# K's bias product at full height inside the warm-up, and the shared low-rank products of gate and up in one group

## The chip, the core and the metric

One core of a Trainium2 chip runs the whole kernel. The metric is the device time of one launch in microseconds (us); every tensor is float32.

## The reference

For x of 2 x 1024 tokens and 512 features, the layer computes

```
xn  = layernorm(x)
Q,K = elu(xn wq^T + bq) + 1,  elu(xn wk^T + bk) + 1        # 16 heads of 32
V   = xn wv^T + bv
att = (Q (K^T V)) / (Q . sum(K) + 1e-8)                    # linear attention
out = x + att wo^T + bo + down(silu(gate(xn)) * up(xn))
gate, up, down = W + shared low rank (sA sB / 8) + experts' low rank (A_e B_e / 8, top 2 of 8 by a router)
```

The hidden width is 1376 = 10 x 128 + 96, the rank 8, and there are 8 experts. The shared low-rank part doesn't depend on the token, so the kernel adds sA sB to the weight itself ("folds" it) and then multiplies once.

## The kernel before, in words

Each engine's order is written out by hand for PE, DVE, ACT and POOL; a line's place in the source is its place in that engine's queue, and an engine runs its queue in order. Only the DMA queue of SP is ordered by the compiler's scheduler. The products are cut up in Strassen's manner (seven products in place of eight), so DVE and POOL build sums of weights and tokens, while PE multiplies. The stages, in order of time:

1. **Start.** PE runs `WARM` = 18 transposes of the identity (L249), while the first tile of x is loaded and normalized. The loop at L667 handles the first two tiles of 128 tokens: `moments` and `deviations` give the mean and 1/sqrt(variance) on DVE, with one square root (`sd`, L268) on ACT; `norm` (L298) writes `xn`; `transpose_x(0)` transposes `xn` on PE (L308) and copies it out of PSUM on ACT (L310). Then comes `pbk`: the row bk is spread over 128 partitions by a product of a column of ones with the row (L676), contracting over 1 row, and ACT copies it back into `bk_sb` (L677). `project_k` (L362) begins K's projection.
2. **K, and K^T times xn** (to about 134 us), for 16 tiles in pairs; the sums `pg` of L401 gather in the four PSUM banks `pg0` to `pg3`.
3. **`query_unit(0)`**: Q of the first batch. Between its products stands `Finish(1)`, which turns the second batch's `pg` into the attention's matrix. Its banks come in turn from `pg0` to `pg3`, by the counter `made`: the products are `pc`, `pr`, `pv`, two `pw` and four `pko` (L553), and ACT copies each `pko` into `gt` (L554). After it the PSUM is given out anew, eight banks in turn, and `shared_factors` transposes the shared factors (`psa`, L560) into `sat`.
4. **`query_unit(1)`**: Q of the second batch, with hooks between its products. `attend(0)` multiplies Q by the spread 1/denominator (L903); `fold_rest(0)` in hook P7 folds gate's part of the 96 last columns (`pfr` L1046 on PE, adds L1049 on DVE). Hook P4 loads the first pair of gate and up weights.
5. **The rest stage** (to about 239 us): `fold_rest(1)` for up, then `rest(b)` for each batch: three products `pr` (L1077 to L1090) of the 96 last columns, with two places for other work between them. `fold(0, 0)` and `fold(0, 1)` stand there: `fold_pe` (L958) multiplies, for four chunks of 128 features, 8 rows of `sat` with 8 rows of sB; `fold_adds` (L967) adds the results to the weights, and `fold_sums` (L971 to L974) builds the Strassen sums. `inner_weight_sums` (`wi`, L1176 to L1179) goes one level deeper.
6. **Ten units** (`unit(j, b)`), then the down projection and attention's output together, to the end.

Two kinds of PE instruction matter. Every float32 product is two passes, each with its own weight load. And where a product contracts over 8 rows only, four of them are placed on four groups of 32 rows (`rows = slice(k * 32, ...)`) and write four banks.

`hold(v)` (L145) is a small memset on DVE ahead of a load: the load then waits for DVE's place in its queue.

Of the kernel before, what the change touches and what calls it, by code (L numbers as in the profile page):

```python
# [15 lines left out]
P = 128  # L16
# [21 lines left out]
def layer_kernel(  # L38
# [23 lines left out]
    nc = tc.nc  # L62
# [10 lines left out]
    RANK = LR // (E + 1)  # L73
# [4 lines left out]
    NC = D // P  # L78
# [8 lines left out]
    REST = DFF - FULL * P  # L87
# [3 lines left out]
    UT = TB // 2  # L91
    NQ = UT // P
    NPQ = NC // 2
    WARM = 18
    NBC = 3

    TILES = [b * TPBATCH + g * TPB + t for b in range(NBATCH) for t in range(TPB) for g in range(2)]
# [1 line left out]
    def by_chunk(w):  # L99
        return w.rearrange("(c p) n -> p c n", p=P)  # L100
# [38 lines left out]
    ident = const.tile([P, P], F32, name="ident")  # L139
# [9 lines left out]
    def load_x(n):  # L149
        x_sb[n] = x_ring[:, n % 4, :]  # L150
        nc.sync.dma_start(out=x_sb[n], in_=x[ts(TILES[n], P), :])

    wk_sb = p1.tile([P, NC, D + E], F32, name="wk_sb")
    load_x(0)
    bk_sb = p1.tile([P, D], F32, name="bk_sb")
    nc.scalar.dma_start(out=bk_sb[0:1, :], in_=bk.unsqueeze(0))
    nc.scalar.dma_start(out=wk_sb[:, :, D:], in_=by_chunk(w_router))
    for c in range(NC):
# [28 lines left out]
    sat = ffn.tile([P, n_sat, P], F32, name="sat")  # L187
# [3 lines left out]
    ones = p1.tile([P, P], F32, name="ones")  # L191
# [3 lines left out]
    for b in range(NBATCH):  # L195
        t = p2.tile([P, 2, NC, 32], F32, name=f"ksd{b}")
# [43 lines left out]
    tags = None  # L240

    def bank(name, shape=None, tag=None):
        tag = tag or (next(tags) if tags else "ps")
        return ps_pool[0].tile(shape or [P, TB], F32, tag=tag, name=name)


    warm = bank("warm", [P, NC, P], "pt")
    for _ in range(WARM):
        nc.tensor.transpose(warm[:, 0, :], ident, ident)  # L249

    def moments(first, n):
        for i in range(first, first + n):
# [4 lines left out]
    def deviations(first, n):  # L257
        variances(first, n)
        reciprocals()
# [42 lines left out]
    def transpose_x(n, tag="pt"):  # L302
        i = TILES[n]
        pt = [bank(f"pt{i}", [P, NC, P], tag)] * 2
        if n == 0:
            pt[1] = bank("pt0_1", [P, NC, P], "ua")
        for c in range(NC):
            nc.tensor.transpose(pt[c // 2][:, c, :], xns[n][:, ts(c, P)], ident)  # L308
        for k in range(2):
            nc.scalar.copy(xnT[i // TPBATCH][k][:, :, ts(i % TPBATCH, P)], pt[k][:, 2 * k : 2 * k + 2, :])  # L310
# [184 lines left out]
    class Finish:  # L495


        def __init__(self, b, pg, ksum):
            self.b, self.pg, self.ksum = b, pg, ksum
            self.made = 0  # L500

        def bank(self, name, shape=None):
            if self.b == 0:
# [163 lines left out]
    for n in range(2):  # L667
        moments(n, 1)
        deviations(n, 1)
        norm(n)  # L670
        load_x(n + 4)
        if n == 0:
            transpose_x(0)

            pbk = bank("pbk", tag="x")
            nc.tensor.matmul(pbk, ones[0:1, :], bk_sb[0:1, :], start=True, stop=True)  # L676
            nc.scalar.copy(bk_sb, pbk)  # L677
    wq_sums, sums1 = query_weight_sums(), token_sums(1)
    sums0 = [take_sums(0, i) for i in range(2)]
    fin = []  # L680
# [18 lines left out]
    def load_weights(t, w):  # L699
        hold(t[:, 0, 0:1])  # L700
        nc.sync.dma_start(out=t, in_=by_chunk(w))
# [38 lines left out]
    tags = cycle(("x", "pt", "ua", "lo"))  # L740
# [146 lines left out]
    def attend(b, g=None):  # L887

        if b:
            todo = [(c, g) for c in range(NC)]  # L890
            by = []
            for c in range(NC):
                rows = slice(c * 32, (c + 1) * 32)
                by.append(bank(f"pb{b}_{g}_{c}"))
                nc.tensor.matmul(by[c], spread[rows, g, :], dens[b][rows, :], start=True, stop=True)
        else:
            k = len(attended)
            attended.extend((k, k + 1))
            todo = [(i % NC, i // NC) for i in attended[-2:]]
            by = [bcs[i] for i in attended[-2:]]  # L900
        for (c, g), t in zip(todo, by):
            v = qt[b, c, g]
            nc.vector.tensor_mul(v, v, t)  # L903
            if b == 0:
                spread_den()

            j, i = c % NPQ, c // NPQ
            nc.sync.dma_start(
                out=q_dram[b][j][:, :, 2 * i + g, :].rearrange("s p n -> p s n"),
                in_=v.rearrange("p (s n) -> p s n", n=UT),  # L910
            )
# [35 lines left out]
                )  # L947
        wsum[j] = (ws, sb)

    def fold_pe(j, i, tags=()):  # L950

        sb = wsum[j][1]
        pf = []
        for k in range(NC):
            rows = slice(k * 32, k * 32 + RANK)
            name = f"pf{i}_{j}_{k}"
            pf.append(spare_bank(tags[k], name) if tags else bank(name))
            nc.tensor.matmul(pf[k][:, 0 : 2 * P], sat[rows, i, :], sb[rows, i, :, :], start=True, stop=True)  # L958
        return pf

    def fold_adds(j, i, pf):

        t = wsum[j][0][i]
        v = t.rearrange("p s (k m) -> p s k m", m=P)
        for k in range(NC):
            at = v[:, k // 2 : k // 2 + 7 : 6, k % 2, :]
            nc.vector.tensor_add(at, at, pf[k][:, 0 : 2 * P].rearrange("p (h m) -> p h m", h=2))  # L967

    def fold_sums(j, i):
        t = wsum[j][0][i]  # L970
        nc.vector.tensor_add(t[:, S1, :], t[:, A21, :], t[:, A22, :])  # L971
        nc.vector.tensor_sub(t[:, S3, :], t[:, A11, :], t[:, A21, :])
        nc.vector.tensor_sub(t[:, S2, :], t[:, S1, :], t[:, A11, :])
        nc.vector.tensor_sub(t[:, S4, :], t[:, A12, :], t[:, S2, :])  # L974
# [19 lines left out]
    tags = None  # L994
# [8 lines left out]
    def token_diffs(b, tag):  # L1003
        xdiff.append(ffn.tile([P, TB], F32, tag=tag, name=f"xdiff{b}"))
        nc.gpsimd.tensor_sub(xdiff[b], xa[b][:, 0:TB], xa[b][:, TB:BT])

    def fold(j, i):
        def f():
            fold_adds(j, i, fold_pe(j, i))
            fold_sums(j, i)  # L1010

        return f

    RA = P // 2
    RB = REST - RA

    def rest_cols(i):

        return slice(i * RA, (i + 1) * RA), slice(P + i * RB, P + (i + 1) * RB)
# [15 lines left out]
                nc.sync.dma_start(out=sb[k * 32 : k * 32 + RANK, i, :], in_=bw[ER:LR, RC])  # L1037
        return t, sb, bd

    def fold_rest(i):  # L1040
        t, sb, _ = w_rest
        pf = []
        for k in range(NC):
            rows = slice(k * 32, k * 32 + RANK)
            pf.append(bank(f"pfr{i}_{k}"))
            nc.tensor.matmul(pf[k][:, 0:REST], sat[rows, i, :], sb[rows, i, :], start=True, stop=True)  # L1046
        for k in range(NC):
            for at, f in zip(rest_cols(i), (slice(0, RA), slice(RA, REST))):
                nc.vector.tensor_add(t[:, k, at], t[:, k, at], pf[k][:, f])  # L1049

    def rest(b, between=(None, None)):
        t, _, bd = w_rest
# [47 lines left out]
    for _ in range(2):  # L1100
# [1 line left out]
    token_diffs(0, "xd")  # L1102
    query_unit(1, {
        "P5": [lambda: attend(0)],
        "P7": [lambda: fold_rest(0), lambda: attend(0)],
        "P3": [lambda: attend(0)],
        "P4": [lambda: attend(0), lambda: load_weights(0, True)],
    })
    load_weights(1)
    def u_tile(name):  # L1110
        return up_.tile([P, TB], F32, tag="u", name=name)

# [37 lines left out]
    def token_sums_1(eng, b):  # L1150

        t = xnT[b][0][:, :, TB:BT].rearrange("p k (h n) -> p k h n", n=TH)
        b11, b21 = tsum[b][1][:, 0], tsum[b][1][:, 1]
        eng.tensor_sub(t[:, 0, 0], b11[:, TH:], b11[:, 0:TH])
        eng.tensor_sub(t[:, 0, 1], b21[:, TH:], t[:, 0, 0])
        eng.tensor_sub(t[:, 1, 0], b21[:, TH:], b11[:, TH:])
        eng.tensor_sub(t[:, 1, 1], b21[:, 0:TH], t[:, 0, 1])
        inner_tokens(b, (1,), lambda i, k: t[:, k // 2, k % 2])
# [309 lines left out]
        return sb, wdr, bd, *diffs  # L1468

    sb_d, wdr, bd_sb, wdr_diff, bd_diff = load_last()  # L1470
    fold_rest(1)
    low_rank_in(2)
    low_rank_in(3)
    denominators(1)
    list(token_sums_56(nc.vector, 0, slot(6, [2, 4, TH], "ti56_0")))
    rest(0, (fold(0, 0), lambda: attend(1, 0)))
    attend(1, 1)
    token_diffs(1, "den")
    token_sums_1(nc.vector, 0)
    rest(1, (fold(0, 1), lambda: list(inner_weight_sums(nc.vector, 0, (1, 5, 6)))))  # L1480
    flush()
    ps8.close()
    p2_stack.close()
# [35 lines left out]
    FREE = ("held0", "held1", "x0", "x1"), ("ab0", "x0", "ab1", "x1")  # L1519

    def next_pair(j):

        pf = {}


        def pe(i):
            return lambda: pf.update({i: fold_pe(j, i, FREE[i])})

        def adds(i):
            return lambda: fold_adds(j, i, pf.pop(i))  # L1530

        def sums(eng, *ps):
            return lambda: list(inner_weight_sums(eng, j, ps))

        last = {}

        def last_sums(n):
            def f():
                g = last.setdefault(0, inner_weight_sums(nc.vector, j, (1, 5, 6)))
                for _ in range(n):  # L1540
                    next(g, None)

            return f

        return (
            {"6c": [pe(0)], "1d": [adds(0)], "6d": [pe(1)], "7": [adds(1)]},
            {"6c": [lambda: fold_sums(j, 0)], "2c": [lambda: fold_sums(j, 1), sums(nc.gpsimd, 3)],
             "3b": [sums(nc.gpsimd, 2), last_sums(2)], "3d": [last_sums(3)]},
        )
# [26 lines left out]
    tags = cycle(("ab0", "ab1", "x0", "x1"))  # L1576
# [590 lines left out]
```

## Time and profile before

| | us |
|---|---|
| median of 3 runs | 726.39 |
| lowest, highest | 724.82, 728.07 |
| the profiled execution | 724.74 |
| its span (what the profile covers) | 722.9 |
| PE busy | 714.9 |
| DVE busy | 579.9 |
| ACT, POOL busy | 198.2, 143.7 |

The profiled execution lasted 1.84 us longer than the span that the profile shows. Times in the profile count from the span's start. A line of the chain of waits has the start, the length, the engine, the tile written and the source line; a line of the timeline has the start, the time from the first to the last of merged instructions, and in brackets how long the engine had been idle and what ended that.

### The profile page before, as it was taken

How to read it: one execution, taken by the hardware profiler on the slowest of the kernel's cores; microseconds unless marked ns; L12 is line 12 of the kernel's file. 1: busy time of each engine (PE TensorE's matmuls, PEld its weight loads, DVE VectorE, ACT ScalarE, POOL GpSimd, SP SyncE). 2: the span in 40 equal slices, each digit the busy share in tenths (PEclk: the TensorE clock that was granted, in tenths of full speed). 3: DMA queues.
4: the chain of work that ended last, by engine and by line, in shares of the span. 5: the costliest groups of instructions: out<-in, count | busy, mean ns of one | idle time of the engine just before them, and what ended most of it. 6: DMA issues, size and time to landing. Idle time of an engine off the chain costs nothing.

```text
span 722.9 us, 9907 instructions
## 1 busy us (share of the span) xinstructions
PE 714.9 (99%) x3428; PEld 491.3 (68%) x3428; DVE 579.9 (80%) x1330; ACT 198.2 (27%) x438; POOL 143.7 (20%) x176
## 2 busy tenths in 40 slices
PE   8999999999999999999999999999999999999998
PEld 6666675454433566567567667566688899899897
DVE  6788766777687688778878878868888889998884
ACT  4434413453442233333333333333200000000000
POOL 4033011101000771311311310544520100000000
PEclk9999999999999999999999999999999999999999
DMA  6343001115585001211201201334653344533101
GB/s 177 99 137 104 0 1 57 42 34 144 131 218 155 19 4 58 88 34 58 88 29 59 88 30 59 117 120 143 204 182 117 117 161 129 158 109 110 59 16 44
DMA packets 61734, 66.85 MB, mean 92 GB/s; under 512 B 10866, under 2 KB 49522, under 8 KB 61428
## 3 DMA queue, kind: packets, MB, share of 16 engines
q1 hardware_dynamic: 61154, 66.20, 29.9%
q8 instruction: 27, 0.44, 0.3%
q14 instruction: 23, 0.19, 0.1%
q10 hardware_dynamic: 530, 0.02, 0.0%
HBM read 44.11 MB, written 22.09 MB: 92 GB/s over the span
## 4 chain that ended last, share of the span: by engine, by line
PE 83%; DVE 13%; ACT 3%; issue 1%; DMA 0%; DVEq 0%
PE ab L1202 16%; PE b L1262 8%; PE po L1942 7%; PE pg L401 5%; PE pya L1771 4%; PE pxa L1771 3%; PE pqu L772 3%; PE pyb L1771 3%; PE ph L1639 3%; PE x L1202 3%; PE pxb L1771 2%; PE pyc L1771 2%; PE pxa L851 2%; PE b L1257 2%; PE pr L1090 2%; PE kua L430 2%
## 5 line engine op out<-in xcount | busy, mean ns | idle before, releaser
L1262 PE MATMUL b<-t,w 128*128 128x512 f32 x160 | 83.2, 601 | 0.8 <-DVE t L1284 0.8
L401 PE MATMUL pg<-kt,xn 128*128 128x512 f32 x128 | 58.7, 594 | 0.5 <-DVE kt L345 0.5
L1284 POOL TENSOR_TENSOR r<-r,r 128x512 f32<-128x512 f32 x20 | 30.1, 1525 | 84.5 <-DVE t L1284 82.9
L1202 PE MATMUL ab<-ti,wi 128*128 128x256 f32 x180 | 45.4, 379 | 0.0
L1202 PEld LDWEIGHTS ab<-ti,w 128*128 128x128 f32 x140 | 25.1, 189 | 29.4 <-DVE r L1230 8.2
L1284 DVE TENSOR_TENSOR r<-r,r 128x512 f32<-128x512 f32 x60 | 44.9, 788 | 0.0
L1202 PEld LDWEIGHTS ab<-ti,wi 128*128 128x128 f32 x180 | 34.2, 190 | 13.2 <-issue 5.0
L1202 PE MATMUL ab<-ti,w 128*128 128x256 f32 x140 | 41.2, 387 | 0.5 <-DVE r L1230 0.2
L401 PEld LDWEIGHTS pg<-kt,xn 128*128 128x128 f32 x128 | 23.2, 190 | 22.6 <-issue 20.6
L1235 ACT COPY r<-ab 128x256 f32<-128x256 f32 x50 | 18.6, 373 | 71.1 <-PE ab L1202 71.1
L1230 DVE TENSOR_TENSOR r<-r,ab 128x256 f32<-128x256 f32 x50 | 20.9, 417 | 20.1 <-ACT r L1227 19.6
L1262 PEld LDWEIGHTS b<-t,w 128*128 128x128 f32 x160 | 29.2, 190 | 11.3 <-issue 5.9
L1238 DVE TENSOR_TENSOR r<-r,ab 128x256 f32<-128x256 f32 x50 | 20.8, 417 | 16.0 <-ACT r L1235 15.7
L1212 ACT COPY r<-ab 128x256 f32<-128x256 f32 x50 | 18.7, 374 | 48.5 <-PE ab L1202 47.1
L1942 PE MATMUL po<-wd,f 128*128 128x256 f32 x140 | 30.9, 380 | 0.1
L410 POOL TENSOR_TENSOR ksum<-ksum,kt 128x512 f32<-128x512 f32 x12 | 15.8, 1318 | 71.7 <-DVE lg L447 42.3
L1223 ACT COPY r<-ab 128x256 f32<-128x256 f32 x50 | 18.6, 373 | 40.8 <-PE ab L1202 40.8
L1942 PEld LDWEIGHTS po<-wd,f 128*128 128x128 f32 x140 | 26.4, 190 | 4.4 <-issue 0.5
L1885 DVE TENSOR_TENSOR f<-f 128x256 f32<-128x256 f32 x84 | 29.3, 417 | 0.1
L1202 PE MATMUL ab<-xnT,w 128*128 128x256 f32 x100 | 29.4, 390 | 0.0
L1202 PE MATMUL ab<-xnT,wi 128*128 128x256 f32 x100 | 28.1, 379 | 0.0
L1202 PEld LDWEIGHTS ab<-xnT,w 128*128 128x128 f32 x100 | 18.1, 189 | 10.8 <-issue 4.5
(482 smaller groups left out, 1652.1 us busy)
## 6 DMA issues: line engine op xcount, KB each, us to landing
h_dram<-h SPq DMA_DIRECT2D x40, 256.0 KB
f<-h_dram SPq DMA_DIRECT2D x10, 512.0 KB
x_ring<-in_x_dram SPq DMA_DIRECT2D x16, 256.0 KB
q_dram<-qt SPq DMA_DIRECT2D x16, 256.0 KB
xr<-in_x_dram SPq DMA_DIRECT2D x16, 256.0 KB
out_dram<-xr SPq DMA_DIRECT2D x15, 256.0 KB
w<-in_w_up_dram SPq DMA_DIRECT2D x10, 256.0 KB
w<-in_w_gate_dram SPq DMA_DIRECT2D x10, 256.0 KB
```

The costliest lines, as they stand in the source:

```text
L401: nc.tensor.matmul(pg[m], xns[n][:, ts(m, P)], kt, start=(j == 0), stop=(j == TPBATCH - 1))
L772: nc.tensor.matmul(banks[c], wqs[p][:, k, ts(c, P)], tsum[b][p][:, k, :], start=(start and k == 0), stop=(k == 1), skip_group_check=True,)
L1202: nc.tensor.matmul(out, w, t, start=start, stop=True, skip_group_check=True)
L1212: nc.scalar.copy(self.r[0][:, H0], self.ua)
L1230: nc.vector.tensor_add(self.r[1][:, H1], self.r[1][:, H1], self.lo)
L1238: nc.vector.tensor_add(self.r[1][:, H0], self.r[1][:, H0], self.lo)
L1262: nc.tensor.matmul(pb[m], ws[m][:, A_OF[p], ts(k, P)], tsum[b][p][:, k, :], start=start, stop=True, skip_group_check=True)
L1284: eng.tensor_add(to[m], t[m], v[m])
L1639: nc.tensor.matmul(phs[u][g * ER : (g + 1) * ER, :], a, f[:, g, :], start=(ns[0] == 0 and n == 0), stop=(last and n == len(chunks) - 1), s ...
L1771: nc.tensor.matmul(o, lhsT, rhs, start=first, stop=True, skip_group_check=True)
L1885: op(t[:, at, :], t[:, x_, :], t[:, y, :])
L1942: nc.tensor.matmul(ps[p][:, q, :], lhsT, rhs, start=start, stop=stop, skip_group_check=True)
```

## The change

- `bk_sb` is filled with zeros by DVE before the row bk is loaded into row 0; `pbk` contracts over all 128 rows, and stands on PE after 13 warm-up transposes, with 3 more behind it, instead of behind `transpose_x(0)`. The copy of `pbk` stands on ACT ahead of the copies of `transpose_x(0)`.
- `Finish` starts its counter at 3: for the second batch `pc` takes `pg3`, `pr` `pg0`, `pv` `pg1`, the two `pw` `pg2` and `pg3`, and `pko` 0 to 3 take `pg0` to `pg3` in this order (before: `pg1`, `pg2`, `pg3`, `pg0`).
- `fold_rest` is done once for gate and up, behind `query_unit(1)`: 8 products in one group into 4 banks, and 8 adds of double width instead of 16.
- The first fold is done once for gate and up in the first place within `rest(0)`; its sums come later on DVE, behind `attend(1, 1)`; `inner_weight_sums` moves from the second place of `rest(1)` to the first.
- `load_weights(1)` gets the four `hold` memsets. In the order that the compiler then gives SP, the loads of the second pair of weights stand behind those of the first, loads of `wdr` and `bd_sb` take the places that they had, and the eight small loads of `sb` for the third pair stand ahead of the second batch's `q_dram` stores.

```diff
-    WARM = 18
+    WARM = 13, 3
...
     bk_sb = p1.tile([P, D], F32, name="bk_sb")
+    nc.vector.memset(bk_sb, 0.0)
     nc.scalar.dma_start(out=bk_sb[0:1, :], in_=bk.unsqueeze(0))
...
-    for _ in range(WARM):
-        nc.tensor.transpose(warm[:, 0, :], ident, ident)
+
+    def warm_up(n):
+        for _ in range(n):
+            nc.tensor.transpose(warm[:, 0, :], ident, ident)
+
+    warm_up(WARM[0])
+
+    pbk = bank("pbk", tag="x")
+    nc.tensor.matmul(pbk, ones, bk_sb, start=True, stop=True)
+    warm_up(WARM[1])
...
-            self.made = 0
+            self.made = NC - 1
...
         if n == 0:
+            nc.scalar.copy(bk_sb, pbk)
             transpose_x(0)
-
-            pbk = bank("pbk", tag="x")
-            nc.tensor.matmul(pbk, ones[0:1, :], bk_sb[0:1, :], start=True, stop=True)
-            nc.scalar.copy(bk_sb, pbk)
...
-    def fold_pe(j, i, tags=()):
+    def fold_pe(j, tags=(), ms=(0, 1)):
...
-            nc.tensor.matmul(pf[k][:, 0 : 2 * P], sat[rows, i, :], sb[rows, i, :, :], start=True, stop=True)
+        for i in ms:
+            for k in range(NC):
+                rows = slice(k * 32, k * 32 + RANK)
+                nc.tensor.matmul(pf[k][:, ts(i, 2 * P)], sat[rows, i, :], sb[rows, i, :, :], start=True, stop=True)
...
-    def fold_rest(i):
+    def fold_rest():
         t, sb, _ = w_rest
-        pf = []
+        pf = [bank(f"pfr{k}", [P, 2, REST]) for k in range(NC)]
+        for i in range(2):
+            for k in range(NC):
+                rows = slice(k * 32, k * 32 + RANK)
+                nc.tensor.matmul(pf[k][:, i, :], sat[rows, i, :], sb[rows, i, :], start=True, stop=True)
         for k in range(NC):
...
+            for at, f in ((slice(0, P), slice(0, RA)), (slice(P, None), slice(RA, REST))):
+                v = t[:, k, at].rearrange("p (i n) -> p i n", i=2)
+                nc.vector.tensor_add(v, v, pf[k][:, :, f])
...
-        "P7": [lambda: fold_rest(0), lambda: attend(0)],
+        "P7": [lambda: attend(0)],
...
-    load_weights(1)
+    load_weights(1, True)
...
-    fold_rest(1)
+    fold_rest()
...
-    rest(0, (fold(0, 0), lambda: attend(1, 0)))
+
+    def first_fold():
+        pf = fold_pe(0)
+        for i in range(2):
+            fold_adds(0, i, pf)
+
+    rest(0, (first_fold, lambda: attend(1, 0)))
     attend(1, 1)
     token_diffs(1, "den")
+    for i in range(2):
+        fold_sums(0, i)
     token_sums_1(nc.vector, 0)
-    rest(1, (fold(0, 1), lambda: list(inner_weight_sums(nc.vector, 0, (1, 5, 6)))))
+    rest(1, (lambda: list(inner_weight_sums(nc.vector, 0, (1, 5, 6))), None))
```

More of the change, by code (lines that the diff above doesn't have):

```diff
@@ L954, in fold_pe @@
         for k in range(NC):
-            rows = slice(k * 32, k * 32 + RANK)
-            name = f"pf{i}_{j}_{k}"
+            name = f"pf{ms[0]}_{j}_{k}"
             pf.append(spare_bank(tags[k], name) if tags else bank(name))
-            nc.tensor.matmul(pf[k][:, 0 : 2 * P], sat[rows, i, :], sb[rows, i, :, :], start=True, stop=True)
+        for i in ms:
+            for k in range(NC):
+                rows = slice(k * 32, k * 32 + RANK)
+                nc.tensor.matmul(pf[k][:, ts(i, 2 * P)], sat[rows, i, :], sb[rows, i, :, :], start=True, stop=True)
         return pf
@@ L966, in fold_adds @@
             at = v[:, k // 2 : k // 2 + 7 : 6, k % 2, :]
-            nc.vector.tensor_add(at, at, pf[k][:, 0 : 2 * P].rearrange("p (h m) -> p h m", h=2))
+            nc.vector.tensor_add(at, at, pf[k][:, ts(i, 2 * P)].rearrange("p (h m) -> p h m", h=2))
     def fold_sums(j, i):
@@ L1005, in token_diffs @@
         nc.gpsimd.tensor_sub(xdiff[b], xa[b][:, 0:TB], xa[b][:, TB:BT])
[L1007 to L1012, printed above, removed]
     RA = P // 2
@@ L1038, in rest_weights @@
         return t, sb, bd
-    def fold_rest(i):
+    def fold_rest():
         t, sb, _ = w_rest
-        pf = []
-        for k in range(NC):
[L1044 to L1049, printed above, removed]
+        pf = [bank(f"pfr{k}", [P, 2, REST]) for k in range(NC)]
[3 more added lines that the diff above has]
+                nc.tensor.matmul(pf[k][:, i, :], sat[rows, i, :], sb[rows, i, :], start=True, stop=True)
+        for k in range(NC):
+            for at, f in ((slice(0, P), slice(0, RA)), (slice(P, None), slice(RA, REST))):
+                v = t[:, k, at].rearrange("p (i n) -> p i n", i=2)
+                nc.vector.tensor_add(v, v, pf[k][:, :, f])
     def rest(b, between=(None, None)):
@@ L1526, in pe @@
         def pe(i):
-            return lambda: pf.update({i: fold_pe(j, i, FREE[i])})
+            return lambda: pf.update({i: fold_pe(j, FREE[i], (i,))})
         def adds(i):
```

## The prediction

> **What bounds the kernel now.** I read the page's busy row and the chain first. PE is busy for 99% of the span, the chain lies on PE for 83%, and DMA has none of it: only what shortens PE's queue, or a wait on that chain, counts.
>
> ```profile
> PE 714.9 (99%) x3428; PEld 491.3 (68%) x3428; DVE 579.9 (80%) x1330; ACT 198.2 (27%) x438; POOL 143.7 (20%) x176
> PE 83%; DVE 13%; ACT 3%; issue 1%; DMA 0%; DVEq 0%
> ```
>
> Then the chain of waits in the three windows that the change touches. At the start it crosses engines:
>
> ```profile
> 6.15 0.67 PE pt L308 x4
> 6.82 1.06 PE pbk L676 x2
> 7.88 0.02 issue
> 7.90 0.59 ACT bk_sb L677
> 8.49 0.11 ACT sd L268
> ```
>
> `sd` of the second tile stands behind the copy of `pbk` on ACT; the timeline has its input `ve` done at 7.96 (7.81 + 0.15), and `sd` starts at 8.38. From there DVE's statistics lead to the first `pg` at 17.18.
>
> Timeline of PE where the PSUM is given out anew, and the chain's two `pd`, and its low-rank groups:
>
> ```profile
> 163.36 1.02 PE L772 MATMUL pqv<-t,wq_sb 128*128 128x512 f32 x2
> 164.73 0.38 PE L560 MATMUL psa<-ident,sa 128*128 128x128 f32 x1 [0.36 <-ACT gt L554]
> ```
> ```profile
> 169.55 1.85 PE pd L873 x16
> ...
> 192.20 0.41 PE pfr L1046 x8
> 192.61 3.63 PE pqu L772 x8
> 196.24 3.43 PE pqv L772 x8
> 199.67 0.41 PE pfr L1046 x8
> 200.08 7.06 PE pxa L851 x16
> 207.15 2.20 PE pd L873 x16
> ...
> 218.28 0.65 PE pf L958 x8
> 218.92 1.05 PE pr L1088 x2
> 219.98 3.43 PE pr L1090 x8
> ```
>
> To see: `psa` waits for the last copy of `gt`; the same 16 passes of `pd` take 2.20 instead of 1.85; and the product behind a low-rank group is 0.20 longer than its like (3.63 to 3.43; 1.05 to two passes of 0.43). So a `pfr` group costs 0.61 in all, a `pf` group 0.84.
>
> **The change part by part.**
>
> *Start.* Removed from PE behind `pt`: 1.06. But the chain goes on through DVE, which gains only what `sd` waited for: 8.38 - 7.98 = **0.40**. PE's side: without `pbk`, K's first 12 passes (2.7 us, 7.80 to 10.53) start when the first `xnT` copy ends (6.59 + 0.37), at 7.0, and end at 9.65, before the next transposes, due at 10.53 - 0.40 = 10.13. Now the cover in the warm-up. The 18 warm transposes start 0.216 apart ((4.10 - 0.42) / 17), those at 10.53 0.11 apart ((0.60 - 0.27) / 3): PE is at half speed there, though the page's clock row reads 9 everywhere. 13 of them end at 4.17; at half speed `pbk` is two passes of 0.86, the three behind it 0.65: `pt` could start at 6.54 instead of 6.15. The Trainium skill ("TensorE: Matmul & The Clock Gate", Part 1) has full rate after about 4 us of sustained activity, give or take 0.5: 5.4 here, `pbk` ends at 5.65 and `pt` isn't late. It speaks against putting work where PE runs at half rate; but 0.39 late makes K's passes end at 10.04, still before 10.13. By the row or by the rule, 0.40.
>
> The zeros: DVE is idle until 3.27; nearest is POOL's memset of 128x640, 0.63. The row's load then issues at about 1.4 instead of 0.74; the 256 KB of x landed 2.5 us after issue, so this row lands by 3.9, before 4.17. Behind it ACT's router load and table load (1.28) end at about 3.7, before `sd` at 4.40. Cost nothing; if the row came later than 4.7 or so, `pt` would be later than the cover allows, one for one.
>
> *Counter.* `psa`'s first bank is `pg0`: last read by the fourth `gt` copy before, by the first one now (162.64 + 0.62). PE's next pass after 163.36 and its follower falls at 164.22; `psa` started at 164.73. Gain between 0.36 (the bracket) and 0.51. The fourth and fifth `psa` then wait for DVE's adds L831 of `pqv` (the second ends at 165.10), where they arrive anyway (164.22 + 0.21 + 7 x 0.11 = 165.2). I take **0.50**. `pc` now waits for the copy of `pg3`, done at 136.2, five us early; `pko`'s fourth has the same wait as before.
>
> *fold_rest.* The first group goes (0.61), the second doubles. Its second half costs columns alone, 2 x 96 at 0.43 per 512 = 0.16, or as the first half, 0.37 to 0.41. The skill ("TensorEngine Tiling (Array Packing)", Key Properties) says that a change of tiling mode drains the array, and that tiles can load weights and multiply in parallel; that would hide the loads: gain 0.45. The row says otherwise: `pf` takes 0.65 for two passes, 0.32 each, where 256 columns are 0.21, so 0.11 of load shows in each pass. Gain **0.22**, the switch alone.
>
> DVE loses eight adds at P7 (1.00 us from 193.71) and does the wide ones behind the holds (0.4 longer than the eight there, 0.93). So `attend` at P7 frees its buffer 0.9 earlier, and the load for which L903 waits 1.73 at 200.76 is issued 0.9 earlier (it follows that buffer: 195.33 on SP). `pd` waits for the last `qt` of DVE behind it (the 0.35); PE arrives 0.22 sooner, DVE 0.9: **0.35**, or 0 if the load doesn't move. The adds then end around 208.5, `pr` L1080 needs the first of them after 209.
>
> *First fold.* The group at 218.28 gets 0.65 longer, the one at 234.75 goes (0.84): **0.20** (0.41 by the rule). DVE does eight adds there (4 take 1.41) instead of four adds and four sums (2.9 us either way), so `pb` behind it waits no longer. They need the up weights: the first pair's 1 MB is issued from 209.6, ahead of the second pair, and DMA moved 270 to 304 GB/s then: landed by about 215, used at 219.5.
>
> *Sums later.* Eight sums (2.96) follow `attend(1, 1)` on DVE; behind them are `token_sums_1`, three `hr` products and `wi`, whose third step PE needs in the first unit (242.31 before, 240.6 now). DVE: 228.5 + 2.96 + 1.46 + 2.1 + 2.3 = 237.3. Free by 3.3 us.
>
> *SP and holds.* Two loads of 0.5 leave the place between `d_dram` and `bc`, two small ones of 0.6 take it: even. Eight `sb` loads (2.8) go ahead of the `q_dram` stores, which wait for DVE at 224 anyway, and end before `wi` overwrites their tile at 235. Four memsets are 0.08 on DVE; their tiles were last read at 196.
>
> Sum: 0.40 + 0.50 + 0.22 + 0.35 + 0.20 = 1.67. The ten units are untouched. The profiled execution, 724.74 (span 722.9 and 1.84 around it), becomes 723.1; it lay 1.65 under the median, so against 726.39 I expect **724.7**. With the bounds (0.36, 0 for `pd`; 0.45, 0.41 for the folds) 1.2 to 2.1.
>
> **The rivals.**
>
> *Given back:* what PE saves at `psa` and `pd` returns as a wait for `bc` or `wT`, whose loads hang on SP's queue (issuing or waiting without a gap from 164.71 to 191.28) and move only with the start. For it: L903's wait of 1.73. Against: two of the three waits are tied to DVE, not to SP. Left are 0.40 + 0.22 + 0.20: 725.6.
>
> *More:* DVE's and POOL's earlier work lifts a stall in the first unit. For it: at 253.25 two adds L1284 take 3.36 beside POOL (0.69 alone), and PE waits 0.8 for the next. POOL's chain can begin 6 us earlier. Against: its fifth step waits for stores of `hr`, so it ends only some 3 us earlier than the shift alone. With 0.8 there, 0.5 in the units behind and the folds at 0.86: 723.0, to 722.
>
> *Slower:* DVE between `attend(1, 1)` and the first unit. POOL's sums L1176 start as soon as the eight sums are done, so ten DVE steps (four token sums, three `hr`, three `wi`) may run against it at up to 1.69 instead of about 0.6 (the 3.36 / 2 above): 10 later at worst. From 3.3 on PE stands still at the first `wi` product, from 5.0 the kernel is slower than before, at the worst 6.7 - 1.7 = 5.0 slower: 731.4. Against: POOL's wait for `hr` leaves DVE alone after four steps.
>
> *Doesn't do what it says:* the two halves of a bank written one after the other by the same row group might not overlap the four groups at all: then a merged group costs 8 x 0.21 more and `pf` loses about 1 us: 725.9. The passes of one group already follow each other in the same bank, so I give it little.
>
> **How the numbers follow.** What a measurement of this kernel can tell from no change is about 0.5%, 3.6 us: below 722.8 is faster, above 730.0 slower. The sum as worked out has 0.62, given back 0.13 (with the last rival), more 0.17, slower 0.08. The runs shown spread by 1.6 to each side. Faster: most of "more" and a small part of the first, 0.20; slower: 0.05 of its case; same 0.75. The range takes the first case with its bounds and the runs' spread, and reaches into "more": 722.0 to 727.0.
>
> **What would show it.** Right: `pbk` before 6.2 and `sd` of the second tile near 8.0; `psa` straight behind `pqv`; `pd` twice about 1.85; one `pfr` group of 16 near 0.8 and one `pf` group near 1.3; PE's first `wi` product without a bracket. Wrong: `pt` later than 6.6; a bracket with `bc`, `wT` or `w` ahead of a PE product between 164 and 245; a first unit that starts less than 1.2 earlier than before.

## The result, and the profile after

The changed kernel takes **722.71 us** (median of 5 runs, 722.40 to 723.49), beside 728.07 (724.82 to 728.35) for the kernel before on the same chip: ratio 0.9941, 95% interval 0.9922 to 0.9959. The prediction was 724.7, in a range of 722.0 to 727.0. The profiled execution took 722.83 (span 721.0); before, 724.74 (722.9). The two profiles differ by 1.9 us and the two medians by 5.4. That gap is the main thing to explain.

The page's busy row and the shares of the chain, after:

```profile
PE 714.4 (99%) x3426; PEld 491.4 (68%) x3426; DVE 578.4 (80%) x1327; ACT 198.3 (28%) x438; POOL 142.6 (20%) x176
PE 85%; DVE 12%; ACT 2%; issue 1%; POOL 0%; DVEq 0%; POOLq 0%
```

PE is busy for only 0.5 us less: most of the 1.9 us is waiting that went. The chain of waits at the start:

```profile
1.37 3.04 PE warm L252 x13
4.40 1.92 PE pbk L257 x2
...
7.02 0.62 PE pt L317 x2
...
7.66 0.38 ACT xnT L319
...
8.09 2.90 PE pk L371 x12
10.98 0.44 PE pt L317 x4
...
17.47 3.70 PE pg L410 x8
```

The start did not pay in this run. Both passes of `pbk` ran at half rate, `pt` came at 7.02, and K's passes instead of DVE's statistics lead to the next transposes (10.98 in the chain, 10.82 in the timeline, where 10.13 was forecast). The first `pg` is 0.29 later than before (17.18). The first tile of x, too, landed 0.18 later than before (3.45 and 3.27), but it is not on this chain: `pt` followed PE's own warm-up.

The chain in the middle:

```profile
161.25 3.43 PE pqv L778 x8
164.69 1.27 PE psa L569 x10
...
169.39 1.85 PE pd L879 x16
...
198.91 0.63 PE pfr L1047 x16
...
206.60 1.85 PE pd L879 x16
...
217.39 1.08 PE pf L966 x16
```

`psa` follows `pqv` without a gap. The second `pd` takes 1.85 (2.20 before). One group of 16 `pfr` takes 0.63, where one of 8 took 0.41. One group of 16 `pf` takes 1.08, where one of 8 took 0.65. So the second half of a merged group costs 0.22 and 0.43. Its columns alone, two passes at 0.43 per 512 columns, are 0.16 and 0.43.

In the first unit another 0.68 went: from the `pf` group to the second `b` product behind it are 5.66 us, before 6.34. The two ends in the chain, before and then after:

```profile
251.26 0.64 PE pf L958 x8
...
257.60 1.12 PE b L1262 x2
```
```profile
249.96 0.68 PE pf L966 x8
...
255.62 1.12 PE b L1265 x2
```

In the page's list of costliest groups, of before and then of after, the wait has left the last column (idle before the engine, and what ended it):

```profile
L1262 PE MATMUL b<-t,w 128*128 128x512 f32 x160 | 83.2, 601 | 0.8 <-DVE t L1284 0.8
```
```profile
L1265 PE MATMUL b<-t,w 128*128 128x512 f32 x160 | 83.2, 601 | 0.1
```

### The profile page after: what moved, and what is told of

It reads as the page before. It is cut to its first block, busy times and chain, and to the rows that moved or that the text cites. A ratio compares the mean times of both kernels' runs of the same rounds, so it can differ in the third digit from the quotient of the medians.

```text
span 721.0 us, 9901 instructions
## 1 busy us (share of the span) xinstructions
PE 714.4 (99%) x3426; PEld 491.4 (68%) x3426; DVE 578.4 (80%) x1327; ACT 198.3 (28%) x438; POOL 142.6 (20%) x176
## 4 chain that ended last, share of the span: by engine, by line
PE 85%; DVE 12%; ACT 2%; issue 1%; POOL 0%; DVEq 0%; POOLq 0%
PE ab L1205 16%; PE b L1265 8%; PE po L1953 7%; PE pg L410 5%; PE pqu L778 4%; PE pya L1782 4%; PE pxa L1782 4%; PE pyb L1782 3%; PE ph L1650 3%; PE x L1205 3%; PE pxb L1782 2%; PE pyc L1782 2%; PE pxa L857 2%; PE b L1260 2%; PE pqv L778 2%; PE pr L1092 2%
## 5 line engine op out<-in xcount | busy, mean ns | idle before, releaser
L1287 DVE TENSOR_TENSOR r<-r,r 128x512 f32<-128x512 f32 x60 | 43.2, 762 | 0.0
```

Source lines behind the costliest of these rows:

```text
L1287: eng.tensor_add(to[m], t[m], v[m])
```

## The experiments

### The kernel before, looked at again

No edit.

> The kernel before, unchanged, with a profile of its own. Half-rate theory (in some runs TensorE stays at half speed past the warm-up and K's first products pay for it): the times spread again over about 724.8 to 728.4, and a profile of a run above 726.5 shows K's first passes (L362) about 0.43 apart instead of 0.22, a first pg later than 17.2. Even theory (the savings seen in the profile are all, the spread lies elsewhere): a slow run's profile has its first pg at 17.2 and loses its time later.

Measured: 726.41 (724.64 to 728.48, 22 runs), ratio 0.9998 (0.9988 to 1.0009). The times are not spread evenly. Of all 86 runs of this kernel in the experiments, 8 lie at 724.6 to 725.1, 39 at 726.1 to 726.7, 39 at 727.8 to 728.7, and none between. So its median depends on how many runs fall in each group (about 726.4 in four sets of runs, 728.1 in two). The profile of before that I had predicted from, at 724.74, is of the smallest group. This profile, at 726.45, is of the middle one. Its chain at the start:

```profile
6.49 0.67 PE pt L308 x4
7.16 1.05 PE pbk L676 x2
8.21 4.51 PE pk L362 x12
...
19.21 3.70 PE pg L401 x8
```

K's 12 passes take 4.51, where the sum had 2.7. The same time in windows (from:to, length, busy time and number of instructions of PE, its weight loads, DVE, ACT and POOL, then the granted clock of PE and two figures of DMA):

```profile
5.59:9.00 3.41, 2.51 (x10) 1.48 (x11) 1.98 (x8) 1.34 (x4) 1.26 (x1) 1.00 1.00 337
9.00:12.42 3.42, 3.42 (x10) 2.62 (x9) 3.16 (x10) 0.20 (x1) 3.39 (x3) 0.50 0.27 72
12.42:15.83 3.41, 3.41 (x19) 2.96 (x18) 1.84 (x8) 1.77 (x5) 0.78 (x3) 1.00 0.32 96
```

The third number from the end is the clock: full for 3.41 us, half for 3.41, full for good. With PE busy throughout, 10 passes fit into the half-rate stretch and 19 into the next. In the full-rate stretch ahead of it PE is busy for only 2.51 us, and the 1.05 of `pbk` are of a product over one row. The page's clock row reads 9 in every slice, as a slice is 18 us.

### A run of the upper group

No edit, one profiled run.

> The kernel before, for a profile of another group of runs. If it is one of the 728 group: the stretch of 3.41 us ahead of 6.2 to 7.7 us holds the idle time ahead of pt and is followed by a second at half rate, full rate comes only at 9.6 to 11.1 or at 13 to 14.5 us, and the first pg starts near 20.5 to 20.8 (17.2 in the 724.7 group, 19.2 in the 726.3 group).

Measured: 728.36, span 726.6. Its chain:

```profile
6.43 1.09 PE pt L308 x4
7.51 2.00 PE pbk L676 x2
9.51 4.89 PE pk L362 x12
...
20.89 3.70 PE pg L401 x8
```

`pt`, `pbk` and most of K's twelve passes are at half rate; the trace has full rate from 13.65. Counted back from there in stretches of 3.41, one runs from 3.41 to 6.82 and has the 0.95 us of idle time ahead of `pt`; the next, 6.82 to 10.24, has the 2.00 of `pbk` over one row. Neither was followed by full rate; the one after it, full of K's products, was. The expectation held, the first `pg` by 0.1 later than its upper end. So in the three profiled runs of this kernel (724.74, 726.45, 728.36) the first `pg` starts at 17.18, 19.21 and 20.89: 2.03 and 1.68 apart. (The runs are 1.71 and 1.91 apart, as the second `pd` takes 2.20, 1.85 and 2.06 in them.) A stretch of 3.41 at half rate can cost 1.7 us of PE's work, and these are the steps between the groups.

### Only the start

The kernel before with the start of the changed kernel (zeros, `WARM = 13, 3`, `pbk` in the warm-up, its copy ahead of `transpose_x(0)`).

> Before, with the start's part of the change alone (zeros, bias product at full height in the warm-up, copy first). Half-rate theory: the long product keeps TensorE busy until the transposes, the spread shrinks to about 1 us and the median falls by 2.5 to 4 us, to about 724 to 725.5, though the profile's first pg lies 0.3 later than in a fast run of before. Even theory: the median rises by 0.3 us and the spread stays.

Measured: 724.57 (723.9 to 725.1, 5 runs), ratio 0.9959 (0.9944 to 0.9974). The groups are gone. In its profile full rate came at 4.97, so that the second pass of `pbk` was already fast; the chain has

```profile
2.12 4.41 DMA x_ring<-in_x_dram
...
7.69 0.21 ACT sd L277
...
8.87 0.93 DVE xn L307
...
16.78 3.70 PE pg L410 x8
```

The first `pg` is 0.40 earlier than before, but the equality with the prediction's step is partly luck. `sd` follows its input (7.51 + 0.16) at once, so the wait of 0.4 is gone; besides, the second tile of x landed 0.32 earlier than in the first profile (6.54; DVE took it at 6.86 there), and `xn` behind it took 0.93 instead of 0.55.

### All but the start

The changed kernel with the start of before.

> The changed kernel, with the start as before (18 transposes, bias product of height 1 behind the first transposes). Half-rate theory: its fast runs are at 722.4 (0.3 below the changed kernel), but runs spread by over 3 us up to about 726, median 724.5 to 726. Even theory: all runs at about 722.4, as tight as those of the changed kernel.

Measured: 724.30 (722.93 to 726.05, 10 runs), ratio 0.9965 (0.9950 to 0.9980). Three groups again, at 722.9 to 723.2, 724.2 to 724.5 and 725.9 to 726.1: each about 2 us under its like of before. So the rest of the change is worth 2 us in every group, and the start is what removes the groups.

### Products in place of transposes in the warm-up

```diff
-    WARM = 18
+    WARM = 9
-        nc.tensor.transpose(warm[:, 0, :], ident, ident)
+        nc.tensor.matmul(warm[:, 0, :], ident, ident, start=True, stop=True)
```

> Before, with 9 real products of the identity in the warm-up instead of 18 transposes (the same 18 passes of 128 columns). If only products count as work for the clock: full speed comes within the warm-up in every run, its later passes are 0.11 apart, the spread shrinks, and the median is at 724 to 725. If transposes count alike, or the spread lies elsewhere: times and spread as before, 724.8 to 728.4.

Measured: 728.00 (724.78 to 728.45, 14 runs), ratio 0.9999 (0.9985 to 1.0013), the same three groups (3, 3 and 8 runs). What kind of work fills the warm-up doesn't matter here.

### Full height at the old place

```diff
+    nc.vector.memset(bk_sb, 0.0)
-            nc.tensor.matmul(pbk, ones[0:1, :], bk_sb[0:1, :], start=True, stop=True)
+            nc.tensor.matmul(pbk, ones, bk_sb, start=True, stop=True)
```

> The kernel before, with bk_sb filled with zeros and pbk contracting over all 128 rows, but at its old place behind transpose_x(0), and 18 warm transposes. Its runs and those of the kernel before fall in three groups (about 724.7, 726.3, 728.0); the profile of a 726 run has TensorE back at half rate for one stretch of 3.41 us after its first 3.41 us at full rate. Theory 'gap' (PE's idle time between the last warm transpose and pt, about 0.7 to 1.0 us, brings the half-rate stretch): height changes nothing, the groups stay, median 726 to 728, ratio 1.000 within 0.002. Theory 'height' (the product over 1 row counts for nothing in the stretch): the 726 group goes to 724.7, the 728 group, whose stretch lies ahead of pbk, stays; fastest runs in most, median 724.7 or 728, hardly a run near 726.3.

Measured: 726.26 (724.71 to 726.80, 10 runs), ratio 0.9975 (0.9965 to 0.9984): 4 runs at 724.7 to 725.5, 6 at 726.2 to 726.8, none at 728. Of before's 15 runs on the same chip 10 were there, 5 at 726.3 to 726.7 and none lower. Neither theory had this. Its profile, at 726.55, says what became of the upper group:

```profile
7.35 1.72 PE pbk L677 x2
...
19.24 3.70 PE pg L402 x8
```

Here, too, PE idled (0.79) ahead of `pt` and `pbk` ran at half rate, but full rate came at 10.36, one stretch after the idle one and not two. A reading that fits both kernels: a product over one row counts in a stretch much like idle time, one over 128 rows counts as work, and too much of the former keeps the clock at half rate or puts it back there. Then the upper group loses its second bad stretch and becomes this one at 726.3, and the old middle group loses its only one.

### No gap ahead of the transposes

```diff
-    WARM = 18
+    WARM = 22
```

> The kernel before with 22 warm transposes in place of 18, so that at half rate they end at about 6.1 us, where pt is due; the bias product stays behind pt and over 1 row. Theory 'gap': the groups at 726.3 and 728.0 go, all runs between 724.5 and 725.5 (pt may be 0.2 late in some), ratio about 0.998. Theory 'height': the 726 group stays, since its stretch holds the 1.05 us of pbk; only the 728 group goes; median 726.3 or 724.7.

Measured: 725.41 (724.76 to 726.41, 5 runs), ratio 0.9969 (0.9957 to 0.9981); 4 of 5 runs at 724.8 to 725.5, none at 728. This is nearer to "gap". The run at 726.41 may be a middle one that kept its bad stretch (the one row counting for nothing); it has no profile. Height and gap each take part.

How much a stretch may hold can be narrowed down from the profiles, by counting stretches of 3.41 us from the moment that full rate came. At half rate, with full-height work or transposes, stretches with up to 0.58 us of idle time (the run with products in the warm-up) were followed by full rate, and those with 0.78 or more (the changed kernel) were not. At full rate, 0.43 of idle time with 1.06 of the product over one row did no harm (this run; the kernel before at 724.74 is alike), while 0.90 and 0.96 with 1.05 brought half rate back, at 726.45 and in the profile of "All but the start". Idle time alone did not: a stretch of the run "The first fold in two places again", below, has as much of it, but its `pbk` is of full height and lies in the warm-up.

```profile
5.95:9.37 3.42, 2.52 (x13) 1.59 (x12) 1.87 (x7) 1.44 (x4) 0.15 (x1) 1.00 0.82 295
9.37:12.78 3.41, 3.41 (x19) 2.70 (x18) 3.20 (x10) 0.80 (x4) 3.33 (x3) 1.00 0.50 101
```

PE is busy for 2.52 here and was for 2.51 in the run at 726.45; there half rate followed, here it did not. That speaks for the height as the other part. It is one profile, and no run changed the two in small steps.

### The product earlier in the warm-up

```diff
-    WARM = 13, 3
+    WARM = 10, 3
```

> The changed kernel with 10 warm transposes ahead of pbk and 3 behind it, in place of 13 and 3. In the changed kernel's profile the clock was at half rate to 7.41 us and pt came at 7.02, 0.7 late, so that K's first passes set the next transposes at 10.98. Here pt can start at about 6.4 at half rate, and the transposes behind K's passes at 10.3 to 10.5. Theory 'late pt costs': 0.3 to 0.5 us less in the runs whose clock opens late, median 722.3, lowest as before (722.4 less 0.1). Theory 'DVE's statistics bound the start in nearly all runs': no difference, 722.7. Rival 'the row is late': bk lands after the tenth transpose, pbk waits, a gap opens on PE and half-rate stretches come back: 723.5 to 726.

Measured: 722.63 (722.28 to 723.34, 5 runs), not to be told from the changed kernel's 722.71. In the timeline of PE the product now waits for its row:

```profile
4.21 2.05 PE L257 MATMUL pbk<-bk_sb,ones 128*128 128x512 f32 x2 [0.45 <-DMA bk_sb<-in_bk_dram]
```

The row lands just before 4.2, not by 3.9 as I had worked out, so 13 transposes are barely the cover that it needs. In this run `pt` still came at 6.79 and the next transposes at 10.43 (7.02 and 10.82 in the changed kernel's timeline), but the second tile of x, which landed at 7.2, set the chain. The effect stays below the spread.

### The counter back at 0

```diff
-            self.made = NC - 1
+            self.made = 0
```

> The changed kernel with the bank counter of Finish at 0 as before. psa then waits for the last copy of gt again: a bracket of about 0.36 at psa, and 0.45 to 0.50 us more in all: 723.2, with psa 0.45 later against the end of pqv. Rival: the wait that it removes is taken up by the next one (the adds of pqv, or SP's loads for pd), then 0 to 0.1 more: 722.8.

Measured: 723.46 (722.69 to 724.04, 6 runs), 0.75 over the changed kernel's median, with spreads of 1.1 and 1.4 us. The timeline is more exact:

```profile
165.14 1.38 PE L569 MATMUL psa<-ident,sa 128*128 128x128 f32 x10 [0.37 <-ACT gt L563]
```

The bracket is back. By the chain, `pxa` behind it moves from 165.96 to 166.53, while the first `pg` moved by only 0.08 (17.47 to 17.55): 0.49 for the counter, as predicted.

### `fold_rest` in two places again

The changed kernel with the old `fold_rest(i)` put back, gate's part in hook P7.

> The changed kernel with fold_rest as before: gate's part in hook P7 of query_unit(1), up's part behind it, 8 products in each. 'Columns alone': the second pfr group costs 0.41 of its own and a switch of about 0.2 behind it, so the stretch from psa to the first pr L1079 gets 0.37 (pfr) + 0.35 (pd back at 2.20) = 0.72 longer: 723.4. 'Row' (the prediction's own): 0.22 + 0.35. Rival: pd stays at 1.85, because it was not DVE's earlier end that moved the load: 0.37 alone, 723.1. In the first unit nothing changes (the first b product still without a bracket) if that gain comes from the first fold.

Measured: 723.26 (722.43 to 724.20, 5 runs). Its chain:

```profile
192.10 0.41 PE pfr L1047 x8
192.50 3.63 PE pqu L778 x8
...
199.57 0.41 PE pfr L1047 x8
...
207.04 1.85 PE pd L879 x16
```

The group at P7 costs 0.41 and the switch behind it 0.20 again, so merging saves 0.61 less the 0.22 of the second half. But `pd` stays at 1.85, with DVE's eight adds back in P7: the rival came true. So look again at the wait of L903 for the load of `bc`, in the list of waits (instruction, releaser: total, times, longest). In the three profiles of before (the first, the run at 726.45 and the run at 728.36) it was

```profile
DVE qt L903 <- DMA bc<-d_dram: 1.7, 1, 1.7
```
```profile
DVE qt L903 <- DMA bc<-d_dram: 0.7, 1, 0.7
```
```profile
DVE qt L903 <- DMA bc<-d_dram: 1.6, 1, 1.6
```

and `pd` took 2.20, 1.85 and 2.06. The runs with this part as before fit in: a wait of 1.5 gave 1.96, of 1.0 to 1.2 gave 1.85; in the changed kernel a wait of 1.3 gave 1.85. The load lands differently from run to run of one kernel, and in these runs it reached PE only from 1.5 on.

### The first fold in two places again

The changed kernel with gate's fold and its sums in the first place of `rest(0)`, up's in the first of `rest(1)`, `inner_weight_sums` in the second.

> The changed kernel with the first fold as before: gate in the first place of rest(0), up in the first of rest(1), each with its sums at once, inner_weight_sums in the second place of rest(1). 'Columns alone': the two groups cost 0.41 more on PE; and the first unit: if the 0.68 there comes from POOL's and DVE's earlier sums of the first fold, it goes as well, with a bracket of 0.6 to 0.8 at the second b product: 1.1 in all, 723.8. Rival: the first unit's gain comes from the shift of DVE's whole queue by fold_rest, then it stays: 0.41 alone, 723.1.

Measured: 723.74 (723.68 to 724.21, 5 runs), 1.03 over the changed kernel's median; 1.1 was expected. The chain shows both terms:

```profile
234.16 0.64 PE pf L966 x8
234.80 1.06 PE pr L1090 x2
...
250.67 0.64 PE pf L966 x8
...
257.00 1.13 PE b L1265 x2
```

From `pf` to the second `b` product are 6.33 us again, as before. So the gain in the first unit comes from the first fold. Why is seen where DVE's two adds `r` lie beside POOL. Timeline of the changed kernel (DVE, then POOL):

```profile
251.96 2.68 DVE L1287 TENSOR_TENSOR r<-r,r 128x512 f32<-128x512 f32 x2
```
```profile
251.12 1.28 POOL L1135 TENSOR_TENSOR ti<-t 128x512 f32<-128x512 f32 x1
252.35 1.73 POOL L1135 TENSOR_TENSOR ti<-t,ti 128x512 f32<-128x512 f32 x1
```

and of the kernel before:

```profile
253.25 3.36 DVE L1284 TENSOR_TENSOR r<-r,r 128x512 f32<-128x512 f32 x2
```
```profile
253.13 1.27 POOL L1132 TENSOR_TENSOR ti<-t,ti 128x512 f32<-128x512 f32 x1
254.36 1.71 POOL L1132 TENSOR_TENSOR ti<-t 128x512 f32<-128x512 f32 x1
```

An add takes 0.69 alone. Each of these four ended 0.55 behind the end of the POOL sum that was running when it began. Before, that sum had begun only 0.12 ahead of the first add, which took 1.69; the second add took 1.75. After, the first add began 0.44 ahead of the end of a sum (251.12 + 1.28) and took 0.99; only the second met a whole one (1.76). The Trainium skill ("SBUF — State Buffer", Who interferes with whom) says that DVE's operations with two inputs in SBUF and POOL's contend for one read port, and that the order of issue decides who is held up. The four durations fit it. POOL is busy for 6.92 of the 7 us from 250 on in both kernels: nothing was freed, the two only met in another phase.

## Why the prediction was right, and where not

The range held the time. From profile to profile the first case is the nearest (723.1 forecast, 722.83 measured). The median of 722.71 lies closer to the rival "more" (723.0) than to the 724.7 of the first case, for a reason that neither had. And the close agreement of the profiles is partly luck: two errors of 0.69 and 0.68 cancel.

**The sum against the profiled run.** Predicted 724.74 - 1.67 = 723.1, measured 722.83. Term by term (the measured ones give 722.77):

| step | predicted | measured in the profile |
|---|---|---|
| start | -0.40 | +0.29 |
| counter, `psa` | -0.50 | -0.45 |
| `fold_rest` | -0.22 | -0.37 |
| `pd` | -0.35 | -0.35 |
| first fold | -0.20 | -0.41 |
| first unit | 0 | -0.68 |
| sum | -1.67 | -1.97 |

- *Start.* The step "by the row or by the rule, 0.40" failed in this run, and the sign "`pt` later than 6.6" showed. At half rate I had `pt` at 6.54; it came at 7.02, as `pbk` began 0.11 later than I had it (at 4.28 in the timeline), and its two passes and the three transposes then took 2.74 instead of 2.37. The clock opened only at 7.41, as the stretch from 0.59 to 4.00 has 0.78 us of idle time, the wait for the identity, and the next one had to do. So the first copy of `xnT` began 0.64 behind `pt`, not 0.44. K's passes ran at full rate, but from 8.09 to 10.82, and the cover ended at 10.13: these 0.69 are the whole miss. In the run of the start alone the clock opened at 4.97, and there the wait of `sd` did go.
- *Counter.* Right in size and in its mechanism: 0.45 and 0.49 in two comparisons.
- *The folds.* The mis-sized term is "0.11 of load shows in each pass". The second half of a group cost 0.43 for `pf`, the columns alone, and 0.22 for `pfr`, 0.06 above them. Here the rule that I weighed and set aside was right (tiles load weights and multiply in parallel), with its 0.41; for `pfr` it gave 0.45, and 0.37 was measured.
- *`pd`.* The number came true, the reason did not. The 0.35 were chance in the one execution that I read: before's own `pd` takes 1.85 to 2.20. Averaged over the seven profiles of before and of the kernels that differ from it in the start alone (excess 0.35, 0.21, 0.11 and four times 0), the stall is 0.10. In the five profiles with the merged `fold_rest` it is always 0, but so it is in the one with `fold_rest` apart; whether the change made it rarer is left open.
- *Doesn't do what it says* is out: 16 passes `pfr` in 0.63 leave no room for groups one after the other. *Given back* is out too: no wait for a load of `bc`, `wT` or `w` stands on the chain from 161 to 262.
- *First unit.* The rival "more" had the place and the 0.8; I gave it 0.17 because POOL's chain would end "only some 3 us earlier than the shift alone". POOL's sums for `wi` ended 3.7 us earlier (240.25; before, 243.94), 2.4 more than PE's own shift, and that sufficed, by a change of phase. Which way the phase would fall I had not worked out, so the gain was luck. "Slower" had its collisions as foreseen, but small: four token sums of DVE beside POOL's sums took 0.42 to 0.67 each, and PE never waited for `wi`.

**From the profile to the median.** I added the 1.65 that the profiled run lay under the median, as if it were noise that both kernels share. It was not. These 1.65 are what a half-rate stretch under K's passes costs. By their times, 78 of the 86 runs of before have such a loss once or twice (one run of each group was profiled), and none of the changed kernel's, which spread over 1.1 us. So the change took this away as well, and 723.1 was the better forecast of the median, too. The start is thus worth far more than its 0.40: by the runs of the start alone, 0.41% or 3.0 us (0.26 to 0.56%; the plain medians are 1.9 apart). The trace that I predicted from could not show it, being of the smallest group; but the spread of its runs, 724.82 to 728.07, was on the table, and I took it for noise. The rule that I cited on the clock spoke of when it opens. I used it for `pbk` only, and did not ask whether PE's idle time ahead of `pt`, with a product over one row behind it, could close it again.

## What to carry to other kernels

Where a short kernel's runs fall into groups, find out which group the profile is of before adding anything to it, and look at the first 15 us for passes that take twice their usual time. Once PE has begun, keep it busy at full height until the real work takes over; in these runs a product over one row did not serve as filler. A stall seen in one execution and ended by a DMA is worth its average over several executions, and one between DVE and POOL can turn on some tenths of a microsecond of phase.

## What the hardware showed that I had not expected

- TensorE's clock fell back to half rate 3.41 us after it had opened, behind a stretch with only 0.9 us of idle time and 1.05 us of a product over one row, and stayed there for 3.41 us although PE was busy throughout (10 passes, then 19 in the same time). The Trainium skill ("TensorE: Matmul & The Clock Gate", Part 1) has the length of the window, 3413 ns, and that it runs free of the kernel's start, and both show here: full rate first came at 4.97 to 13.65 us in the profiles. But it has the clock drop after a whole idle window; here 1.95 of 3.41 us sufficed if the product over one row is counted as idle. The 0.90 of idle time alone did not, in the one profile that has it.
- Executions of the same kernel differ in how many of these stretches they lose: none, one or two in the three profiles of before. That goes with three sharp times (724.7, 726.3, 728.1) and hardly anything between.
- The clock column of a window begins with the first change on record: it reads 1.00 for the warm-up, whose transposes run 0.216 apart, twice the later 0.11. The passes' own spacing is the safer sign.
